# A new order for the last 30 microseconds of a fused four-layer kernel: last product by rows, bias products first, gamma and beta on VectorE in one go

## The chip, the cores and the metric

The kernel runs on one core of one Trainium2 chip, as one program that computes four layers for a batch of eight sequences of 512 rows and 512 features in float32. The metric is device time in microseconds (us); a kernel's time is the median of its runs, and lower is better. Engines are called as the profile calls them: PE is TensorE (PEld its weight loads), DVE is VectorE, ACT is ScalarE, POOL is GpSimd, SP is SyncE, from whose queue the transfers are issued.

## The reference, cut to what matters

The first two layers (a grid stencil step, and an attention block with its MLP) are not touched by the change. The third layer is an expert MLP with a norm, the fourth a low-rank response with a gate over the whole sequence:

```python
def L2(x, Wi, bi, Wo, bo, gamma, beta):            # weights of the sequence's expert
    h = gelu(x @ Wi + bi)                          # 512 x 2048
    r = h @ Wo + bo + x                            # 512 x 512
    y = (r - mean(r)) * rsqrt(var(r) + 1e-12)      # over the features of a row
    return y * gamma + beta

def L3(y, safety, U, V, safety_bias, gate_w1, gate_b1, gate_w2, gate_b2, resp_w, resp_b):
    basis = gram_schmidt(U) @ gram_schmidt(V).T
    pooled = y.mean(axis=rows)                     # one vector for the sequence
    h1 = relu(pooled @ gate_w1.T + gate_b1)
    strength = sigmoid(h1 @ gate_w2.T + gate_b2) * sigmoid(safety) * knob
    feats = (y @ basis) @ basis.T[:, :32]          # 512 x 32
    return y + strength * (feats @ resp_w.T + resp_b + safety_bias)
```

Strength needs the mean over all 512 rows of a sequence, so no row of a sequence's output can be finished before its last row has been normalised.

## The kernel before, in words

The whole program is one `fused_kernel`. Stages follow one another: grid, attention, and `mlp_stage` (L1145 on), which holds all that the change touches. `mlp_stage` runs sixteen steps `q` (L1713): steps 0 to 7 are the MLP of the second layer, one sequence each, steps 8 to 15 the expert MLP of the third. A sequence's 512 rows lie as 128 partitions times four rows (`R` = 4), so that its tile `xs[q]` is 128 x 4 x 512.

Both products of a step are Strassen-like schemes of seven block products in float32. Every product of a 128x128 weight tile with a moving tile of 256 columns shows in the profile as two passes. In `run` (L1463) the first product's seven blocks are made for each of four groups of hidden columns (`NG`), slots 0 to 27; the second product's seven blocks follow through `second` (L1536), each accumulated over all four groups in one PSUM tile, at slots 28, 32, ... 52. The block at slot 52 (`p4`, tile name `y_{q}_52`) is the last and is added to rows 2 and 3, columns 0 to 255, of x (`x_add(1, 0, p4)`). In `second` the loop over groups `g` is outside and the loop over the two row blocks `m` inside, so that both rows are complete only at its end.

The order on every engine is that of the Python code, kept by `pin`; nothing reorders it later. Work of other steps is woven in by `hooks`: `at(hooks, s, f, ...)` has f called at slot s. The fourth layer of sequence `q - 1` is made in this way during step q: `tail_norm` (L1600, normalises rows in place), `tail_turn` (L1618, PE transposes of 128x128 blocks and an ACT read that applies gamma and beta as columns and sums over the rows for the gate's mean), `tail_gamma` (L1609), `tail_feats` (L1640: features `pf`, and their copy `ft`), `gate` (L1652: `pg` and h1), `strength` (L1665: `pz`, a sigmoid and the product with the safety score), `add_beta` (on POOL), `tail_sum` (L1679: response `po`) and `tail_add` (L1689: the sum into x, and after rows 1 and 3 a store of two rows).

Sequence 15 has no step behind it. Its rows 0 and 1 are complete before the last block product and get norm, transposes, features and gamma at slots 49 to 55 (L1764 to L1770). Rows 2 and 3 are done behind the loop (L1773 to L1801): beta of rows 0, 1 on POOL; norm of rows 2, 3 together; the gate's products `pg` of the first half; transposes; gamma on DVE; features and gate alternating for the four column blocks; copies and h1 on DVE; beta of rows 2, 3 on POOL; for each row a response product `po` of two parts, `ft` with `rw` and a row of ones with the biases `rb`; strength; and four sums on DVE with two stores of 512 KB.

PSUM tiles come from two rings: tag `tr` with two buffers and tag `u` with six. `rstd_of` (L66) takes one DVE add and one power on POOL.

Of the kernel before, what the change touches and what calls it, by code (L numbers as in the profile page):

```python
# [24 lines left out]
R = 4  # L25
# [1119 lines left out]
def mlp_stage(tc, a, small, xp, io, wo8, x1d, ident, eidx, sigs, layernorm, rstd_of, phalf, wl3, g2, b1, first):  # L1145
# [19 lines left out]
    with ExitStack() as ctx:  # L1165
# [6 lines left out]
        def mm(out, lhsT, rhs, start, stop):  # L1172
            pin(nc.tensor.matmul(out, lhsT=lhsT, rhs=rhs, start=start, stop=stop))  # L1173

        def tp(out, src, idn=ident):
            pin(nc.tensor.transpose(out, src, idn))  # L1176

        def add(out, x, y, op=ALU.add):
            pin(nc.vector.tensor_tensor(out, x, y, op))  # L1179
# [283 lines left out]
        def run(q, hooks):  # L1463
# [9 lines left out]
            def act_quad(g, i, j):  # L1473

                return acts[g][:, 2 * j : 2 * j + 2, H * i : H * i + H]
# [60 lines left out]
            def second(s, A, B, each=None):  # L1536
                y = ps.tile([P, 2, H], F32, name=f"y_{q}_{s}", tag="u", bufs=6)
                for g in range(NG):
                    go(s + g)
                    if s == 28 and g == 2:  # L1540
                        s13(NG - 1)
                    for i in range(2):
                        for m in range(2):
                            mm(
                                y[:, m, :], A(g)[:, i, m * P : (m + 1) * P], B(g)[:, i, :],
                                g + i + m == 0, g + i + m == NG + 1,
                            )
                    if each:
                        each(g)
                return y  # L1550

            def x_add(i, j, t):
                o = quad(x, i, j)
                add(o, t, o)

            def b(i, j):
                return lambda g: quad(wo[g], i, j)
# [25 lines left out]
            add(yu, p7, yu)  # L1583
            x_add(1, 1, yu)
            x_add(1, 0, yu)
            p4 = second(52, lambda g: act_quad(g, 1, 1), b(1, 0))
            x_add(1, 0, p4)

        def t13(q, g):

# [46 lines left out]
                )  # L1637
                t["ys"][c] = y

        def tail_feats(q, rows):  # L1640
            ys = outs[q]["ys"]
            pf = ps.tile([P, P], F32, name=f"pf_{q}_{rows[0]}", tag="tr")
            for c in range(KC):
                for i, r in enumerate(rows):
                    mm(
                        pf[r * RK : (r + 1) * RK, :], wl3[:, c, :], ys[c][:, i, :],
                        c == 0, c == KC - 1,
                    )
            m = slice(rows[0] * RK, (rows[-1] + 1) * RK)
            pin(nc.vector.tensor_copy(outs[q]["ft"][m, :], pf[m, :]))  # L1650

        def gate(q):  # L1652

            pooled = outs[q]["pooled"]
            if len(pooled) > 1:
                add(pooled[0], pooled[0], pooled[1])
            pg = ps.tile([P, 1], F32, name=f"pg_{q}", tag="tr")
            for c in range(KC):
                mm(pg, gw1[:, c, :], pooled[0][:, c : c + 1], c == 0, c == KC - 1)
            h1 = small.tile([P, 1], F32, name=f"h1_{q}", tag="h1")  # L1660
            pin(nc.vector.tensor_scalar(h1, pg, 1.0 / S, gb1, ALU.mult, ALU.add))
            pin(nc.vector.tensor_scalar(h1, h1, 0.0, None, ALU.max))
            outs[q]["h1"] = h1

        def strength(q):  # L1665
            pz = ps.tile([P, 1], F32, name=f"pz_{q}", tag="tr")
            mm(pz, gw2, outs[q]["h1"], True, True)
            st = small.tile([P, 1], F32, name=f"st_{q}", tag="st")
            pin(nc.scalar.activation(st, pz, AF.Sigmoid, bias=gb2))
            add(st, st, sigs[:, q - NB : q - NB + 1], ALU.mult)  # L1670
            outs[q]["st"] = st
# [5 lines left out]
            gadd(x, x, beta[:, None, :].to_broadcast([P, R, D]))  # L1677

        def tail_sum(q, r):  # L1679
            last = q == NQ - 1  # L1680
            ft, m = outs[q]["ft"], slice(r * RK, (r + 1) * RK)
            po = outs[q]["po", r] = ps.tile(
                [P, D], F32, name=f"po_{q}_{r}", tag="u", bufs=6
            )
            mm(po, ft[m, :], rw[m, :], True, not last)
            if last:
                mm(po, ones[m, :], rb[m, :], False, True)

        def tail_add(q, r):  # L1689
            x, t = xs[q], outs[q]  # L1690
            pin(
                nc.vector.scalar_tensor_tensor(
                    x[:, r, :], t["po", r], t["st"], x[:, r, :], ALU.mult, ALU.add
                )
            )
            if r % 2:
                nc.sync.dma_start(
                    a["out"][q - NB].rearrange("(p r) f -> p r f", r=R)[:, r - 1 : r + 1, :],
                    x[:, r - 1 : r + 1, :],
                )  # L1700


        def at(hooks, s, f, *args):
            hooks.setdefault(s, []).append(lambda: f(*args))
# [8 lines left out]
        for q in range(NQ):  # L1713
# [50 lines left out]
            if q == NQ - 1:  # L1764
                half = range(0, 2)
                at(hooks, 49, tail_norm, q, half)
                for c in range(KC):
                    at(hooks, 51 + c, tail_turn, q, half, [c])
                at(hooks, 55, tail_feats, q, half)
                at(hooks, 55, tail_gamma, q, half)  # L1770
            run(q, hooks)

        q, half = NQ - 1, range(2, 4)  # L1773
        x, beta, t = xs[q], extra[q][1][2], outs[NQ - 1]
        gadd(x[:, 0:2, :], x[:, 0:2, :], beta[:, None, :].to_broadcast([P, 2, D]))
        tail_norm(q, half)
        pg = ps.tile([P, 1], F32, name=f"pg_{q}", tag="u", bufs=6)
        for c in range(KC):
            mm(pg, gw1[:, c, :], t["pooled"][0][:, c : c + 1], c == 0, False)
        tail_turn(q, half, range(KC))  # L1780
        tail_gamma(q, half)
        pf = ps.tile([P, P], F32, name=f"pf_{q}_2", tag="u", bufs=6)
        for c in range(KC):
            for i, r in enumerate(half):
                mm(
                    pf[r * RK : (r + 1) * RK, :], wl3[:, c, :], t["ys"][c][:, i, :],
                    c == 0, c == KC - 1,
                )
            mm(pg, gw1[:, c, :], t["pooled"][1][:, c : c + 1], False, c == KC - 1)
        m = slice(half[0] * RK, (half[-1] + 1) * RK)  # L1790
        h1 = small.tile([P, 1], F32, name=f"h1_{q}", tag="h1")
        pin(nc.vector.tensor_copy(t["ft"][m, :], pf[m, :]))
        pin(nc.vector.tensor_scalar(h1, pg, 1.0 / S, gb1, ALU.mult, ALU.add))
        pin(nc.vector.tensor_scalar(h1, h1, 0.0, None, ALU.max))
        t["h1"] = h1
        gadd(x[:, 2:4, :], x[:, 2:4, :], beta[:, None, :].to_broadcast([P, 2, D]))
        for r in range(R):
            tail_sum(q, r)
        strength(q)
        for r in range(R):  # L1800
            tail_add(q, r)  # L1801


# [86 lines left out]
```

## Time and profile before

| | |
|---|---|
| time, median of 3 runs | 2748.12 us (2746.18 to 2751.13) |
| time of the profiled execution | 2746.39 us |
| span of the profile | 2744.6 us |
| PE busy | 2693.7 us, 98% |
| DVE, ACT, POOL busy | 69%, 38%, 55% |
| mean granted clock of PE | 0.994 |
| begin of the last block product's first pass behind the transposes | 2714.03 us |
| last block product complete | 2722.59 us |
| first and last store of sequence 15 issued | 2739.48, 2740.8 us |

Times inside the profile count from the start of the span. The span covers the instructions of one execution; the time of that execution is 1.8 us longer. The granted clock is the share of its full speed that PE is given in a stretch of time. In the chain that ended last, each piece waited for the piece before it.

### The profile page before, as it was taken

The numbers are of one execution on the slowest core, as the hardware profiler recorded it, in microseconds if no ns is written. First come the engines' busy times: TensorE is split into PE (matmuls) and PEld (weight loads), VectorE is DVE, ScalarE is ACT, GpSimd is POOL, SyncE is SP. The second block draws the span as 40 slices with busy tenths as digits, with TensorE's granted clock in tenths as the row PEclk, the third lists the DMA queues.
The fourth block names the chain that finished last, engine by engine and source line by source line (L and its number), as shares of the span: only waits on it lengthen the run. The fifth ranks groups of instructions, "written<-read, shape, count | busy, mean of one in ns | idle before, by whom it ended". The sixth has DMA issues, their size and how long they took to land.

```text
span 2744.6 us, 39872 instructions
## 1 busy us (share of the span) xinstructions
PE 2693.7 (98%) x14662; PEld 2007.0 (73%) x14662; DVE 1899.7 (69%) x3506; ACT 1034.0 (38%) x2196; POOL 1505.3 (55%) x1091
## 2 busy tenths in 40 slices
PE   7999999999999998999999999999999999999998
PEld 4455555555555555888888888888888888888886
DVE  7888888888888655677656756665456566566564
ACT  2576767667667765211211211211121221221221
POOL 3455555555555653565555656646546636636633
PEclk9999999999999999999999999999999999999998
DMA  8765767666675544642543344253133143143120
GB/s 318 238 222 178 246 190 232 220 194 227 195 242 180 170 155 142 192 129 54 143 143 84 96 145 124 55 173 123 44 127 131 51 150 128 53 150 103 63 70 31
DMA packets 190208, 405.27 MB, mean 148 GB/s; under 512 B 24024, under 2 KB 28704, under 8 KB 183742
## 3 DMA queue, kind: packets, MB, share of 16 engines
q1 hardware_dynamic: 186202, 391.97, 42.7%
q0 software_dynamic: 3360, 10.68, 3.2%
q8 instruction: 117, 1.92, 0.3%
q14 instruction: 77, 0.63, 0.1%
q10 hardware_dynamic: 452, 0.07, 0.0%
HBM read 366.97 MB, written 31.50 MB: 145 GB/s over the span
## 4 chain that ended last, share of the span: by engine, by line
PE 92%; DVE 4%; ACT 2%; DMA 1%; issue 1%; SPq 0%; ACTq 0%; POOL 0%; DVEq 0%
PE u L1173 28%; PE y L1173 28%; PE tr L570 8%; PE s L567 5%; PE ctx L567 4%; PE pq L567 4%; PE pv L567 4%; PE o L567 4%; PE pk L567 3%; PE btr L1176 1%; DVE bt L1005 1%; PE xb L570 1%; DVE x L695 1%; PE ytr L1176 1%; ACT bt L1010 1%
## 5 line engine op out<-in xcount | busy, mean ns | idle before, releaser
L982 POOL TENSOR_TENSOR bt<-bt,mk 128x1024 f32<-128x1024 f32 x256 | 542.6, 2141 | 56.8 <-DMA bt<-in_bias 38.2
L1173 PE MATMUL y<-wo,act 128*128 128x256 f32 x2560 | 573.3, 380 | 0.0
L1173 PEld LDWEIGHTS y<-wo,act 128*128 128x128 f32 x2560 | 481.3, 190 | 70.0 <-issue 6.9
L1010 ACT ACTIVATE bt<-bt,mn 128x512 f32<-128x512 f32 x512 | 365.7, 716 | 78.6 <-DVE mn L1005 78.0
L570 PEld LDWEIGHTS tr<-ident,bt 128*128 128x128 f32 x2048 | 229.1, 141 | 153.0 <-issue 124.7
L1005 DVE CUSTOM_DVE_ANT_0 bt<-s,bt 128x512 f32<-128x512 f32 x512 | 330.8, 684 | 2.4 <-PE s L567 2.4
L1173 PE MATMUL u<-bt,wi 128*128 128x256 f32 x1440 | 330.5, 379 | 0.0
L1179 DVE TENSOR_TENSOR act<-u,u 128x512 f32<-128x512 f32 x256 | 173.3, 686 | 210.0 <-PE u L1173 132.6
L1173 PEld LDWEIGHTS u<-bt,wi 128*128 128x128 f32 x1440 | 273.5, 190 | 37.2
L570 PE MATMUL tr<-ident,bt 128*128 128x128 f32 x2048 | 276.2, 278 | 11.5 <-ACT pt L1033 9.4
L1173 PE MATMUL u<-tb,ws 128*128 128x256 f32 x1024 | 242.2, 379 | 0.0
L1033 ACT COPY pt<-tr 128x512 f32<-128x512 f32 x315 | 177.1, 581 | 159.6 <-PE tr L570 155.7
L1173 PE MATMUL y<-t,s 128*128 128x256 f32 x1024 | 234.2, 380 | 0.0
L1182 POOL TENSOR_TENSOR t<-wo,t 128x512 f32<-128x512 f32 x64 | 106.6, 1681 | 200.6 <-PE y L1173 200.5
L1173 PEld LDWEIGHTS u<-tb,ws 128*128 128x128 f32 x1024 | 194.3, 190 | 26.6 <-DVE tb L1179 0.2
L1031 DVE COPY pt<-tr 128x512 f32<-128x512 f32 x197 | 135.7, 689 | 112.7 <-PE tr L570 98.0
L1173 PEld LDWEIGHTS y<-t,s 128*128 128x128 f32 x1024 | 191.1, 190 | 24.1
L1493 ACT ACTIVATE act<-act,b 128x512 f32<-128x512 f32 x128 | 82.9, 712 | 292.9 <-DVE act L1179 292.9
L1493 ACT ACTIVATE act<-act,bi 128x512 f32<-128x512 f32 x128 | 83.8, 712 | 282.6 <-DVE act L1179 282.6
L1179 DVE TENSOR_TENSOR x<-y,x 128x512 f32<-128x512 f32 x96 | 64.5, 685 | 159.1 <-PE y L1173 105.2
L1179 DVE TENSOR_TENSOR u<-u,u 128x512 f32<-128x512 f32 x192 | 131.3, 684 | 58.2 <-PE u L1173 58.1
L567 PE MATMUL s<-kt,qt 32*128 32x512 f32 x1024 | 166.4, 640 | 2.5 <-DVE mn L1005 1.6
(316 smaller groups left out, 4250.1 us busy)
## 6 DMA issues: line engine op xcount, KB each, us to landing
bt<-in_bias SPq DMA_DIRECT2D x256, 512.0 KB
wo<-in_W SPq DMA_DIRECT2D x32, 1024.0 KB
wi<-in_Wi SPq DMA_DIRECT2D x32, 1024.0 KB
wo<-in_Wo_e SPq DMA_DIRECT2D x32, 1024.0 KB
wi<-in_W SPq DMA_DIRECT2D x28, 1024.0 KB
gq<-coef_q SPq DMA_DIRECT2D x21, 512.0 KB
x1d<-x SPq DMA_DIRECT2D x8, 1024.0 KB
x<-x1d SPq DMA_DIRECT2D x8, 1024.0 KB
```

Of the source, the lines that this page charges most:

```text
L567: pin(nc.tensor.matmul(out, lhsT=lhsT, rhs=rhs, start=start, stop=stop))
L570: pin(nc.tensor.transpose(out, src, ident))
L982: nc.gpsimd.tensor_tensor(bt, bt, mask[b, r][:, None, :].to_broadcast([P, 2, S]), ALU.add)
L1005: nc.vector.tensor_tensor_reduce(bt[:, i, :], ss[h], bt[:, i, :], -1.0, 3.0e38, ALU.add, ALU.min, mn)
L1010: nc.scalar.activation(bt[:, i, :], bt[:, i, :], AF.Exp, bias=mn, scale=-1.0, accum_out=sums[b, c, r][:, h : h + 1],)
L1031: pin(nc.vector.tensor_copy(pt[:, :, r % 2, :], tr))
L1033: pin(nc.scalar.copy(pt[:, :, r % 2, :], tr))
L1173: pin(nc.tensor.matmul(out, lhsT=lhsT, rhs=rhs, start=start, stop=stop))
L1176: pin(nc.tensor.transpose(out, src, idn))
L1179: pin(nc.vector.tensor_tensor(out, x, y, op))
L1182: pin(nc.gpsimd.tensor_tensor(out, x, y, op))
L1493: nc.scalar.activation(acts[g][:, k, :], acts[g][:, k, :], func, bias=bi[:, j : j + 1])
```

## The change

The end of step 15 is written anew as `last_row`, in the order in which rows become complete.

- The last block product runs row by row: the loop over `m` is outside, `last_row(m, y)` follows each, and each row has a PSUM tile of 128x256.
- Row 2 gets sum and norm behind the first half; row 3 behind the second.
- The transposes of rows 0, 1 for the third and fourth column block come one slot after the second, both at slot 53. Features of rows 0, 1 are moved behind the product, after row 2's transposes.
- The four bias products (`ones` with `rb`) open the accumulation of `po` ahead of row 3's transposes; the four products of `ft` with `rw` close it behind `pz`.
- Two PSUM tiles hold the transposes of rows 2 and 3 for two column blocks each, and one ACT read takes a column block of both rows.
- gamma and beta for all four rows are two DVE operations of 128x2048, behind row 3's transposes. POOL has no part in it.
- h1 (a Relu), the copy of `ft` and row 0's product with strength are on ACT; row 0's sum is on POOL, rows 1, 2, 3 are summed on DVE.
- Three stores from SP: rows 1 and 2, row 3, row 0.

For the other sequences `tail_sum`, `gate`, `strength` and `tail_feats` do what they did.

```diff
@@ -1583,8 +1583,21 @@
             add(yu, p7, yu)
             x_add(1, 1, yu)
             x_add(1, 0, yu)
-            p4 = second(52, lambda g: act_quad(g, 1, 1), b(1, 0))
-            x_add(1, 0, p4)
+            if q < NQ - 1:
+                p4 = second(52, lambda g: act_quad(g, 1, 1), b(1, 0))
+                x_add(1, 0, p4)
+            else:
+                for m in range(2):
+                    y = ps.tile([P, H], F32, name=f"y_{q}_52_{m}", tag="u", bufs=6)
+                    for g in range(NG):
+                        if g % 2 == 0:
+                            go(52 + 2 * m + g // 2)
+                        for i in range(2):
+                            mm(
+                                y, act_quad(g, 1, 1)[:, i, m * P : (m + 1) * P],
+                                b(1, 0)(g)[:, i, :], g + i == 0, g + i == NG,
+                            )
+                    last_row(m, y)
 
         def t13(q, g):
 
@@ -1637,9 +1650,9 @@
                 )
                 t["ys"][c] = y
 
-        def tail_feats(q, rows):
+        def tail_feats(q, rows, tag="tr", bufs=2):
             ys = outs[q]["ys"]
-            pf = ps.tile([P, P], F32, name=f"pf_{q}_{rows[0]}", tag="tr")
+            pf = ps.tile([P, P], F32, name=f"pf_{q}_{rows[0]}", tag=tag, bufs=bufs)
             for c in range(KC):
                 for i, r in enumerate(rows):
                     mm(
@@ -1652,8 +1665,6 @@
         def gate(q):
 
             pooled = outs[q]["pooled"]
-            if len(pooled) > 1:
-                add(pooled[0], pooled[0], pooled[1])
             pg = ps.tile([P, 1], F32, name=f"pg_{q}", tag="tr")
             for c in range(KC):
                 mm(pg, gw1[:, c, :], pooled[0][:, c : c + 1], c == 0, c == KC - 1)
@@ -1662,9 +1673,11 @@
             pin(nc.vector.tensor_scalar(h1, h1, 0.0, None, ALU.max))
             outs[q]["h1"] = h1
 
-        def strength(q):
+        def strength(q, also=None):
             pz = ps.tile([P, 1], F32, name=f"pz_{q}", tag="tr")
             mm(pz, gw2, outs[q]["h1"], True, True)
+            if also:
+                also(*range(R))
             st = small.tile([P, 1], F32, name=f"st_{q}", tag="st")
             pin(nc.scalar.activation(st, pz, AF.Sigmoid, bias=gb2))
             add(st, st, sigs[:, q - NB : q - NB + 1], ALU.mult)
@@ -1677,14 +1690,11 @@
             gadd(x, x, beta[:, None, :].to_broadcast([P, R, D]))
 
         def tail_sum(q, r):
-            last = q == NQ - 1
             ft, m = outs[q]["ft"], slice(r * RK, (r + 1) * RK)
             po = outs[q]["po", r] = ps.tile(
                 [P, D], F32, name=f"po_{q}_{r}", tag="u", bufs=6
             )
-            mm(po, ft[m, :], rw[m, :], True, not last)
-            if last:
-                mm(po, ones[m, :], rb[m, :], False, True)
+            mm(po, ft[m, :], rw[m, :], True, True)
 
         def tail_add(q, r):
             x, t = xs[q], outs[q]
@@ -1697,6 +1707,100 @@
                 nc.sync.dma_start(
                     a["out"][q - NB].rearrange("(p r) f -> p r f", r=R)[:, r - 1 : r + 1, :],
                     x[:, r - 1 : r + 1, :],
+                )
+
+        q15 = NQ - 1
+        z = {}
+
+        def last_row(m, y):
+            x, r, t = xs[q15], 2 + m, outs[q15]
+            gamma, beta = extra[q15][1][1:]
+            o = x[:, r, 0:H]
+            add(o, y, o)
+            st = small.tile([P, 6], F32, name=f"z_st_{r}", tag="ln2_st")
+            mv = z["mv", r] = small.tile([P, 2], F32, name=f"z_mv_{r}", tag="ln2_mv")
+            pin(nc.vector.bn_stats(st, x[:, r, :]))
+            pin(nc.vector.bn_aggr(mv, st))
+            rs = z["rs", r] = rstd_of(mv[:, 1:2], LN_EPS2, 1, "ln2", pin)
+
+            def scaled():
+                pin(
+                    nc.vector.tensor_scalar(
+                        x[:, r, :], x[:, r, :], mv[:, 0:1], rs, ALU.subtract, ALU.mult
+                    )
+                )
+
+            if m == 0:
+                scaled()
+                return
+            z["tr"] = [
+                ps.tile([P, 2, 2, P], F32, name=f"ytr_{q15}_2_{c}", tag="tr") for c in range(2)
+            ]
+            last_turn(0)
+            tail_feats(q15, range(0, 2), "u", 6)
+            for k in range(R):
+                po = t["po", k] = ps.tile([P, D], F32, name=f"po_{q15}_{k}", tag="u", bufs=6)
+                mm(po, ones[k * RK : (k + 1) * RK, :], rb[k * RK : (k + 1) * RK, :], True, False)
+            scaled()
+            last_turn(1)
+            pg = ps.tile([P, 1], F32, name=f"pg_{q15}", tag="u", bufs=6)
+            for c in range(KC):
+                mm(pg, gw1[:, c, :], t["pooled"][0][:, c : c + 1], c == 0, False)
+            cols, ys = extra[q15][2], []
+            pool = small.tile([P, KC], F32, name="z_pool", tag="pool")
+            for c in range(KC):
+                v = ap.tile([P, 2, P], F32, name=f"yT_{q15}_2_{c}", tag="tmp", bufs=4)
+                pin(
+                    nc.scalar.activation(
+                        v, z["tr"][c // 2][:, c % 2, :, :], AF.Identity, bias=cols[:, 1, c : c + 1],
+                        scale=cols[:, 0, c : c + 1], accum_out=pool[:, c : c + 1],
+                    )
+                )
+                ys.append(v)
+            tail_gamma(q15, range(R))
+            add(x, x, beta[:, None, :].to_broadcast([P, R, D]))
+            pf = ps.tile([P, P], F32, name=f"pf_{q15}_2", tag="u", bufs=6)
+            for c in range(KC):
+                for i in range(2):
+                    r = 2 + i
+                    mm(
+                        pf[r * RK : (r + 1) * RK, :], wl3[:, c, :], ys[c][:, i, :],
+                        c == 0, c == KC - 1,
+                    )
+                mm(pg, gw1[:, c, :], pool[:, c : c + 1], False, c == KC - 1)
+            h1 = small.tile([P, 1], F32, name=f"h1_{q15}", tag="h1")
+            pin(nc.scalar.activation(h1, pg, AF.Relu, bias=gb1, scale=1.0 / S))
+            pin(nc.scalar.copy(t["ft"][2 * RK :, :], pf[2 * RK :, :]))
+            t["h1"] = h1
+
+            def response(*rows):
+                for r in rows:
+                    m = slice(r * RK, (r + 1) * RK)
+                    mm(t["po", r], t["ft"][m, :], rw[m, :], False, True)
+
+            strength(q15, response)
+            out = a["out"][q15 - NB].rearrange("(p r) f -> p r f", r=R)
+            v = ap.tile([P, D], F32, name="z_r", tag="tmp", bufs=4)
+            pin(nc.scalar.mul(v, t["po", 0], t["st"]))
+            gadd(x[:, 0, :], x[:, 0, :], v)
+            for r in (1, 2, 3):
+                pin(
+                    nc.vector.scalar_tensor_tensor(
+                        x[:, r, :], t["po", r], t["st"], x[:, r, :], ALU.mult, ALU.add
+                    )
+                )
+            pin(nc.sync.dma_start(out[:, 1:3, :], x[:, 1:3, :]))
+            pin(nc.sync.dma_start(out[:, 3, :], x[:, 3, :]))
+            pin(nc.sync.dma_start(out[:, 0, :], x[:, 0, :]))
+
+        def last_turn(m):
+            for c in range(KC):
+                tp(
+                    z["tr"][c // 2][:, c % 2, m, :],
+                    xs[q15][:, 2 + m, c * P : (c + 1) * P],
                 )
 
@@ -1765,40 +1869,8 @@
                 half = range(0, 2)
                 at(hooks, 49, tail_norm, q, half)
                 for c in range(KC):
-                    at(hooks, 51 + c, tail_turn, q, half, [c])
-                at(hooks, 55, tail_feats, q, half)
-                at(hooks, 55, tail_gamma, q, half)
+                    at(hooks, (51, 52, 53, 53)[c], tail_turn, q, half, [c])
             run(q, hooks)
-
-        q, half = NQ - 1, range(2, 4)
-        x, beta, t = xs[q], extra[q][1][2], outs[NQ - 1]
-        gadd(x[:, 0:2, :], x[:, 0:2, :], beta[:, None, :].to_broadcast([P, 2, D]))
-        tail_norm(q, half)
-        pg = ps.tile([P, 1], F32, name=f"pg_{q}", tag="u", bufs=6)
-        for c in range(KC):
-            mm(pg, gw1[:, c, :], t["pooled"][0][:, c : c + 1], c == 0, False)
-        tail_turn(q, half, range(KC))
-        tail_gamma(q, half)
-        pf = ps.tile([P, P], F32, name=f"pf_{q}_2", tag="u", bufs=6)
-        for c in range(KC):
-            for i, r in enumerate(half):
-                mm(
-                    pf[r * RK : (r + 1) * RK, :], wl3[:, c, :], t["ys"][c][:, i, :],
-                    c == 0, c == KC - 1,
-                )
-            mm(pg, gw1[:, c, :], t["pooled"][1][:, c : c + 1], False, c == KC - 1)
-        m = slice(half[0] * RK, (half[-1] + 1) * RK)
-        h1 = small.tile([P, 1], F32, name=f"h1_{q}", tag="h1")
-        pin(nc.vector.tensor_copy(t["ft"][m, :], pf[m, :]))
-        pin(nc.vector.tensor_scalar(h1, pg, 1.0 / S, gb1, ALU.mult, ALU.add))
-        pin(nc.vector.tensor_scalar(h1, h1, 0.0, None, ALU.max))
-        t["h1"] = h1
-        gadd(x[:, 2:4, :], x[:, 2:4, :], beta[:, None, :].to_broadcast([P, 2, D]))
-        for r in range(R):
-            tail_sum(q, r)
-        strength(q)
-        for r in range(R):
-            tail_add(q, r)
 
 # ---- launch: one core; inputs are laid out here and nothing more ----
```

## The prediction

> **What bounds the kernel now.** I read four views of the profile, from the whole to the end. The page's first parts say that TensorE (PE) is busy for 98% of a span of 2744.6 us, and the chain of work that ended last lies on PE for 92%. The built order of instructions on each engine is the same in both kernels up to the last product of step 15 (the block `y_52`), but for line numbers. So about 2714 us of the span stay as they are, and only the last 30 us can change. The second view is that chain over the end:
>
> ```profile
> 2719.65 1.00 PE pf L1173 x16
> 2720.65 1.94 PE y L1173 x8
> 2722.59 0.02 issue
> 2722.61 0.70 DVE x L1179
> ...
> 2725.33 0.72 POOL ln_r L71
> ...
> 2726.07 0.56 DVE x L85
> ...
> 2726.76 0.85 PE ytr L1176 x2
> ...
> 2732.91 0.57 PE pf L1173 x4
> 2733.47 0.52 PE pg L1173 x2
> 2733.99 3.11 PE po L1173 x16
> ...
> 2739.42 1.32 DVE x L1692 x2
> ```
>
> The columns are start, length and piece of the chain. The last product ends at 2722.59; then a chain of dependent steps runs through all engines: x gets the product, norm (4.0 us), transposes, features and gate alternating on PE (2729.64 to 2733.99), sixteen passes of the response `po`, strength, four sums. In that chain nothing overlaps.
>
> The third view, busy time by stretch, is cut where the granted clock can change (PE's busy time is the second number, the clock is the third from the end):
>
> ```profile
> 50.07:53.48 3.41, 3.41 (x33) 3.41 (x32) 1.82 (x4) 1.15 (x2) 0.00 (x0) 1.00 0.49 194
> 53.48:56.90 3.42, 3.42 (x18) 3.42 (x18) 2.11 (x8) 0.00 (x0) 1.05 (x1) 0.50 0.88 282
> ...
> 1063.82:1067.23 3.41, 2.37 (x20) 1.93 (x18) 2.94 (x7) 2.19 (x6) 1.20 (x1) 1.00 0.02 5
> ...
> 2722.69:2726.10 3.41, 0.67 (x6) 0.58 (x6) 2.45 (x7) 0.00 (x0) 2.62 (x2) 1.00 0.00 0
> 2726.10:2729.51 3.41, 2.37 (x8) 1.26 (x8) 0.97 (x2) 1.52 (x5) 0.00 (x0) 0.50 0.02 5
> 2729.51:2732.93 3.42, 3.42 (x21) 2.17 (x22) 1.23 (x1) 0.89 (x4) 1.95 (x1) 0.50 0.00 0
> ```
>
> PE has 0.67 us of work in the stretch of the norm (2722.69); from its end on it runs at half clock, to 2736.34. The rows from elsewhere are for the question of when that happens. Four passes of `pf` take 0.57 us there; sixteen take 1.00 at full clock (2719.65), so four take 0.25.
>
> The fourth view is the timeline and the groups by shape, for prices:
>
> ```profile
> 2722.41 0.95 PE L1173 MATMUL pg<-pool,gw 128*128 128x1 f32 x8
> 2738.01 2.73 DVE L1692 SCALAR_TENSOR_TENSOR x<-po,st,x 128x512 f32<-128x512 f32 x4
> 2739.48 1.65 SPq L1697 DMA_DIRECT2D out<-x  x2
> ...
> L1613 DVE TENSOR_TENSOR x<-x,gamma 128x2048 f32<-128x2048 f32 x7 | 23.5, 3363 | 0.0
> L1613 DVE TENSOR_TENSOR x<-x,gamma 128x1024 f32<-128x1024 f32 x2 | 2.4, 1216 | 2.6 <-PE ytr L1176 2.6
> L245 DVE TENSOR_TENSOR e<-ce,f 128x2048 f32<-128x2048 f32 x1 | 2.3, 2292 | 0.0
> ```
>
> **The change part by part.** All times below are on the scale of the profiled execution.
>
> *Last product.* The order is `m` outside `g`, but it is still 32 passes at 0.2165 us (1.73 for 8 in the chain). The first two transposes of rows 0 and 1 stand where they stood, so I start at 2714.03, the begin of `y_52`. 32 passes take 6.92, the two remaining pairs of transposes 0.44 (0.22 each): row 2 is complete at 2717.93 and row 3 at 2721.39. Before it was 2722.59: `pf` (1.00 and 0.2 of switching) has left the front of it. **−1.2 us.** No DMA moves here: the stores of step 14 are issued at 2707 as before.
>
> *Row 2* gets its sum and norm from 2717.93 to about 2720.9 under row 3's product (slack 0.5 us). It costs nothing; without this cover it would be the 3.0 us of the next part.
>
> *Row 3's norm.* A sum of 128x256 (0.42, the row of the 128x256 sums of `hT`), one bn_stats (0.71), one aggregate (0.18), 0.18 for v, 0.07 + 0.72 for the power on POOL, 0.56 for the scaling, and gaps of 0.02 to 0.03: 2.97, ending at 2724.36. Before: 4.03. **−1.05 us.** VectorE copies `ft` of rows 0, 1 ahead of the scaling and waits for `pf`; PE does transposes (0.44) and `pf` (1.0 to 1.2) from 2721.39, so the copy ends at about 2723.35, while POOL's power ends at 2723.7. Slack 0.3 us; queued behind are scaling and all that follows, so a later `pf` would count one to one.
>
> *PE in the meantime.* The four bias products of `po` take 1.07 (the eight passes at 2699.57 in the chain of step 14), to 2724.1. PE then waits 0.3 us for the scaling. Four transposes of row 3: 0.66 to the last result, 2725.1.
>
> *The clock.* Does it still fall? In the stretch 2722.69 to 2726.10 the new kernel has 1.4 us of `pf` and bias products, 0.66 of transposes and 0.8 of `pg`: 2.85 us, an estimate from the rows above. Elsewhere the half clock followed on stretches with 1.06 and 1.33 us of PE work and not on those with 2.28 and 2.37. But it also followed on the stretch at 50.07 with 3.41 us, all of the embedding's products (L145, 8 columns wide): narrow products seem not to count, and `pg` is one column wide. Without it 2.05 us are left, nearer to 2.28 than to 1.33: I take the full clock. The Trainium skill speaks against it ("TensorE: Matmul & The Clock Gate", Part 4): a PE transpose doesn't count as busy in the same way; then only 1.4 us count, and the clock falls. The trace doesn't bear that out: the stretch at 1063.82 holds nothing but transposes on PE, 2.37 us, and the clock stays. By the row the clock costs nothing; by the rule it falls at 2726.1, at +1.3 us (rival B).
>
> *ScalarE path.* The first read of the turned tile starts 0.5 us after row 3's first transpose: 2724.95. Four reads at 0.56 (2727.70 to 2728.26 before), the last with its accumulator done 0.64 after its start: 2727.27. PE's features and gate for each column block (0.25 + 0.2) fit under the pitch of 0.56; the last ends at 2727.8. Relu (0.26), `pz` (0.33), sigmoid (0.27) with hand-overs: strength ready for VectorE at 2728.9. The `ft` copy (0.29) lies beside `pz`. The response's eight passes (1.07) run behind `pz`, to 2729.6. Before, from scaling to strength: 11.1 us; now 4.5. The skill advises relu, add and mul on VectorE ("ScalarE: Activation LUTs", Rules for kernel authors). The rows: 0.26 for a one-column ScalarE read against 0.22 + 0.15 for VectorE's two. On VectorE they would stand in front of beta and cost 0.3 to 0.7 of its path, which is the longer one, as follows.
>
> *Gamma and beta, all rows, on VectorE.* They wait for row 3's transposes (they overwrite x): 2725.1. Two ops over 128x2048. Bounds: 2.29 (L245, POOL idle) and 3.36 (L1613 with POOL at work). POOL has nothing from 2723.7 on, so 2.29 each: to **2729.7**. This is later than strength by 0.8: VectorE, not PE, now sets the end. Before, half of this lay under the last product, and beta on POOL.
>
> *Last sums.* Strength times safety, then the first sum starts 0.27 later (2737.74 to 2738.01): 2729.98. Rows 1, 2 are done 1.41 later (2739.42 less 2738.01): 2731.39. Row 3: 2732.05. Row 0: ScalarE's product 0.72, then POOL's sum 1.27 (alone) to 1.80 (beside VectorE's), done at 2732.1 to 2732.6.
>
> *Stores.* Before: issued at 2739.48, 0.06 behind the second sum; data for 2.6 us, end of span at 2744.6, 5.12 later. Now the first 512 KB go at 2731.45, the rows 3 and 0 behind it while data still flow: the third store's data can start at about 2733.4 and the first's end near 2733.6. So the bytes set the end again: 2731.45 + 5.12 = **2736.6**.
>
> *Sum.* Start of the first store 2739.48 to 2731.45: −8.0 us of 2744.6. By term: −1.2 product, −1.05 norm, and −5.8 from scaling to first store (13.0 now less in clock, order and bias products: 2726.62 to 2739.48 is 12.86, 2724.36 to 2731.45 is 7.09). The profiled execution took 2746.39 with a span of 2744.6 and would take 2738.4. The median shown is 2748.12, 1.7 above; less 8.0: **2740.1** (−0.29%).
>
> **The rivals.**
> A, forecast: VectorE sets the end at full clock, −8.0.
>
> B, the clock halves all the same. For it: 2.05 is below every stretch that held, and at 2729.51 even 3.42 us of busy PE did not bring the full clock back. Against: the row of transposes. Price, if it falls at 2726.1: the last three pairs of features and gate at 1.09 instead of 0.45, so strength at 2731.0 and the first sum at 2731.3, +1.3. Falling earlier would need a stretch that takes in more of the dense product; falling at 2727 costs +0.7. So −6.7: 2741.4; bounds −7.3 and −6.1.
>
> C, gamma and beta cost 3.36 each as in steps 9 to 15. For it: most L1613 rows; against: POOL is at work in those. +2.1: −5.9, 2742.2.
>
> D, slower than before: the phase of the clock's stretches. They run free, by the same page (Part 1); no run here shows it yet. The half clock comes in pieces of 3.41 us, and near the changes of stage (53 to 145 us and 1050 to 1090 us) there are stretches with PE work between 2.15 and 2.7 us. If another phase closes more of them, each costs about 1.7 us (half of 3.41), anywhere in the kernel. It decides from 5 more closed windows on; six give +2.2: 2750.3. Against: three runs before lie within 5 us.
>
> E, the change saves only the product's reorder, since each later piece waits for `pf` behind PE: then −3: 2745.1. Against: 0.3 us of slack, and no DMA in between.
>
> **How the numbers follow.** A 0.66, B 0.17, C 0.07, E 0.06, D 0.04. The likeliest gives 2740.1. A's own range is 2738 to 2742: the medians move by 1 to 2 us, and sizes by 1 us. The range takes B and C in: 2737.0 to 2744.0, which leaves out D, E and the far edges. The bound of what a measurement can tell is 0.2%, 5.5 us: A is beyond it in most draws (0.60 of 0.66), B and C in 0.17 of 0.24; faster 0.77, within 0.19, slower 0.04.
>
> **What would show it.** Clock 1.00 up to about 2729; row 3's product ending near 2721.4; `pf` of rows 0, 1 behind it; VectorE's gamma and beta at 2.29 each, and the first sum waiting for VectorE and not for strength; the first store near 2731.5. A half clock from 2724 or 2726, gamma of 3.3 us, or a scaling that waits for the `ft` copy would make it wrong.

## The result, and the profile after

| | before | changed |
|---|---|---|
| time, median | 2749.7 us (20 runs, 2746.18 to 2752.0) | 2744.99 us (20 runs, 2740.75 to 2748.7) |
| ratio | | 0.9982, 95% interval 0.9976 to 0.9989 |
| span of the profile | 2744.6 us | 2744.7 us |
| first pass of the last block product | 2713.86 us | 2717.69 us |
| from there to the end of the span ("end stretch") | 30.75 us | 27.04 us |

The changed kernel is faster by 0.18%, or 4.9 us (0.0018 of 2749.7). The forecast was 8.0 us and a time between 2737.0 and 2744.0; the time measured lies above that range, and its distance from before is just inside the 0.2% that was given as the bound of what can be told.

The two spans are equal although the time differs, because the work ahead of the end stretch, the same instructions in both, took 3.8 us longer in this profile. That part is left to the end of this text; until then times count from the first pass of the last block product (2713.86 before, 2717.69 after), where it doesn't matter. On that scale the forecast was 22.7 us, and 3.7 of the 8.0 us came.

The chain that ended last, of the changed kernel (start, length, piece):

```profile
2720.02 5.20 PE y L1173 x24
2725.21 0.02 issue
2725.24 0.43 DVE x L1179
...
2727.46 0.56 DVE x L1731
2728.02 0.04 issue
2728.06 0.66 PE ytr L1176 x4
2728.72 0.79 PE pg L1173 x8
2729.51 0.34 PE pf L1173 x4
2729.85 0.31 PE pg L1173 x2
...
2732.48 0.58 PE pz L1173 x2
2733.06 2.10 PE po L1173 x8
2735.16 0.73 DVE x L1791
```

Up to the transposes all is as forecast. Then PE is in the chain without a break, and the eight closing passes of `po` take 2.10 us, where eight took 1.07 in step 14 of the kernel before:

```profile
2699.57 1.07 PE po L1173 x8
```

Busy time by stretch says why (PE's busy time is the second number, the clock the third from the end):

```profile
2725.24:2728.65 3.41, 3.05 (x34) 1.85 (x32) 2.19 (x6) 0.05 (x1) 0.55 (x1) 1.00 0.02 5
2728.65:2732.04 3.39, 3.39 (x33) 2.54 (x31) 3.25 (x2) 2.24 (x8) 0.00 (x0) 1.00 0.00 0
2732.04:2735.45 3.41, 2.69 (x11) 1.01 (x10) 1.80 (x3) 1.13 (x4) 0.00 (x0) 0.50 0.00 0
```

The forecast asked about a stretch from 8.83 to 12.24 on the common scale. In this profile the stretches are cut elsewhere, at 7.55, 10.96 and 14.35. The clock held behind the first of these rows and fell behind the second, right before `pz`, after 3.39 us in which PE was never idle. The timeline of the last operations:

```profile
2728.76 2.29 DVE L1626 TENSOR_TENSOR x<-x,gamma 128x2048 f32<-128x2048 f32 x1 [0.75 <-PE ytr L1176]
...
2731.08 2.29 DVE L1179 TENSOR_TENSOR x<-x,beta 128x2048 f32<-128x2048 f32 x1
...
2733.39 0.16 DVE L1179 TENSOR_TENSOR st<-st,sigs 128x1 f32<-128x1 f32 x1
2735.10 0.69 ACT L1787 ACTIVATE z_r<-po,st 128x512 f32<-128x512 f32 x1 [1.74 <-PE po L1173]
2735.14 2.07 DVE L1791 SCALAR_TENSOR_TENSOR x<-po,st,x 128x512 f32<-128x512 f32 x3 [1.59 <-PE po L1173]
2735.86 1.26 POOL L1182 TENSOR_TENSOR x<-x,z_r 128x512 f32<-128x512 f32 x1 [8.44 <-ACT z_r L1787]
2736.58 0.33 SPq L1795 DMA_DIRECT2D out<-x  x1
```

VectorE is through with beta at 2733.37 and has strength at 2733.55, and then waits 1.59 us for `po`. The first store is at 2736.58, or 18.9 on the common scale; 17.6 was forecast. But from it to the end of the span are 8.1 us, where there were 5.1 before. SyncE's own waits, and the rows of the program's last line in the changed kernel (durations in ns, min/median/max, then first and last start):

```profile
SPq L1958 <- PEq L1958: 3.3, 2, 2.8
...
L1958 POOLq DRAIN  x3: 46/107/8085, 2735.8 to 2744.5; - x3
L1958 SPq DRAIN  x3: 7/7/7, 2741.3 to 2744.2; - x3
```

and the same rows before, with POOL's last operation there:

```profile
2730.98 2.34 POOL L1182 TENSOR_TENSOR x<-x,beta 128x1024 f32<-128x1024 f32 x1 [4.95 <-DVE x L1613]
...
L1886 POOLq DRAIN  x3: 46/107/9165, 2730.9 to 2744.3; - x3
L1886 SPq DRAIN  x3: 7/7/7, 2743.8 to 2744.1; - x3
```

All engines meet at a barrier at the end of the program, each behind a drain of its own work. SyncE, which waits for the stores, drains at 2741.3 in the changed kernel, then no engine does any work for 2.6 us. The view puts this wait down to PE, which had drained long before (its longest drain took 2.5 us from 2732.8). The late one is POOL: its drain began at 2735.8 and took 8.1 us, to 2743.9, that is 6.8 us beyond the end of its last sum (2735.86 + 1.26 = 2737.12). Before, it is the same 6.8 us (2730.9 + 9.17 = 2740.1, last work done at 2733.32), but there the stores ended later and hid it.

### The profile page after: what moved, and what is told of

Its sections match the earlier page's. It is cut to its first block, busy times and chain, and to the rows that moved or that the text cites. A ratio compares the mean times of both kernels' runs of the same rounds, so it can differ in the third digit from the quotient of the medians.

```text
span 2744.7 us, 39871 instructions
## 1 busy us (share of the span) xinstructions
PE 2694.8 (98%) x14662; PEld 2005.6 (73%) x14662; DVE 1906.5 (69%) x3504; ACT 1034.7 (38%) x2199; POOL 1501.9 (55%) x1091
## 4 chain that ended last, share of the span: by engine, by line
PE 93%; DVE 3%; ACT 1%; DMA 1%; issue 0%; SPq 0%; ACTq 0%; POOL 0%; DVEq 0%
PE u L1173 28%; PE y L1173 28%; PE tr L570 8%; PE s L567 5%; PE ctx L567 4%; PE pq L567 4%; PE pv L567 4%; PE o L567 4%; PE pk L567 3%; PE btr L1176 1%; PE l L251 1%; DVE bt L1005 1%; ACT bt L1010 1%; DVE x L695 1%; PE xb L570 1%; PE ytr L1176 1%
## 5 line engine op out<-in xcount | busy, mean ns | idle before, releaser
L1179 DVE TENSOR_TENSOR x<-y,x 128x512 f32<-128x512 f32 (+1 forms) x97 | 64.6, 680 | 158.1 <-PE y L1173 104.2
```

## The experiments

Two theories had to be told apart from their rivals: that POOL's drain ends the program (against: three stores end late by themselves), and that the sums waited for `po` at half clock (against: VectorE's gamma and beta set the end, as forecast). All end stretches are from the first pass of the last block product. (Two of the expectations count from its place in the chain, 0.16 us later, and so give 30.6 and 26.9 for 30.75 and 27.04.)

### The changed kernel again

No edit.

> The changed kernel once more, as the neighbour of the others on the same chip. Measured is the end stretch: from the first pass of the last block product to the end of the span (before 30.6 us, changed 26.9 us in the first profile). Theory (POOL's drain at the end of the program sets the end, and the clock fell before pz and po): POOL's drain ends 6.8 us behind POOL's last sum, SyncE is through with the stores 2 to 3 us earlier, end stretch 25.5 to 27. Rival (three stores with a slow end of their own): SyncE itself is through only shortly before the span's end. If the half clock comes at another place because the clock's stretches run free, po's closing products take 1.1 us instead of 2.1 and the first store is 1 us earlier, but the end stretch shrinks by as much only if POOL's sum moves too. The part ahead of the stretch is longer by about 1.7 us for each further 3.41 us at half clock.

Time 2745.61 us, ratio 0.9982 (0.9975 to 0.9990). End stretch 27.05 us; first store at 18.89; SyncE drained at 23.58; POOL's last sum ended at 19.45 and its drain at 26.24. All of it is within 0.01 us of the first profile, and the clock fell at the same place, before `pz`. The end stretch is a far sharper measure than the time.

### All sums on VectorE

```diff
-            v = ap.tile([P, D], F32, name="z_r", tag="tmp", bufs=4)
-            pin(nc.scalar.mul(v, t["po", 0], t["st"]))
-            gadd(x[:, 0, :], x[:, 0, :], v)
-            for r in (1, 2, 3):
+            for r in (1, 2, 3, 0):
```

> Row 0's sum on VectorE behind rows 1, 2, 3; no ScalarE product and no POOL sum at the end. Theory (POOL's drain): POOL's last work is then row 3's power, about 9 us earlier, its drain is hidden under the stores; VectorE takes 0.66 us more, the last store goes 0.5 us later; end stretch 2.3 us shorter than the changed kernel's (about 24.5 at the same clock). Rival (the stores end late of themselves): the end stretch is the changed kernel's or 0.5 us longer. Time against before: 0.26% faster by the theory, 0.17% by the rival.

Time 2740.34 us, ratio 0.9970 (0.9959 to 0.9982). POOL's last work and the drains of this run:

```profile
2722.03 0.56 POOL L71 TENSOR_TENSOR ln_r<-ln_v,mhalf 128x1 f32<-128x1 f32 x1 [2.90 <-DVE ln_v L69]
...
L1955 POOLq DRAIN  x3: 46/107/7380, 2722.0 to 2737.9; - x3
L1955 SPq DRAIN  x3: 7/7/7, 2737.3 to 2737.6; - x3
```

POOL's drain ends at 2729.4, again 6.8 us behind its last work, and is hidden under the stores; the span ends 0.8 us after SyncE's drain. End stretch 25.32: 1.7 us less than the changed kernel, where 2.3 were expected. The clock accounts for what is missing: here it fell at 12.9 and not at 14.35, in the middle of features and gate, and strength came 0.9 us later (16.6 and not 15.7), although up to there the instructions are those of the changed kernel. In spite of that and of 0.66 us more on VectorE the end is earlier. The rival, no gain, is out.

### POOL last in the kernel before

```diff
         for r in range(R):
             tail_add(q, r)
+        late = small.tile([P, 1], F32, name="late", tag="late", bufs=1)
+        gadd(late, x[:, 3, 0:1], x[:, 3, 0:1])
```

> The kernel before with one more POOL operation of one column, behind the last sum on VectorE; nothing waits for it. Theory (POOL's drain takes 6.8 us from its last work, whatever that is): POOL ends about 2741.0 on the scale of the profile before, its drain 2747.8, where SyncE is through at 2743.8: end stretch +3.9 us (34.5), time +0.14%. Rival (the drain goes by the size of the last operation, or the drain in the changed kernel was late for another reason): 0.2 us of work leaves a short drain, end stretch within 0.5 us of the 30.6 before, time the same.

Time 2753.61 us, ratio 1.0015 (1.0008 to 1.0022).

```profile
2745.07 0.19 POOL L1182 TENSOR_TENSOR late<-x 128x1 f32<-128x1 f32 x1 [8.39 <-DVE x L1692]
...
L1888 POOLq DRAIN  x3: 46/107/7008, 2745.0 to 2752.6; - x3
L1888 SPq DRAIN  x3: 7/7/7, 2747.9 to 2752.3; - x3
```

An addition of one column, 0.19 us long, makes the kernel slower by 4 us. No work waits for it: the second store follows the first by 1.3 us, as before. Its drain ends at 2752.0 (2745.0 + 7.0), 6.8 us behind it; SyncE had drained at 2747.9. The end stretch is 35.64, 4.9 longer than before: 4.1 are the drain, 0.8 the clock, which in this run fell so that `pz` was slow too. The drain doesn't go by the size of the last operation: it is 6.8 us behind 128x1024, 128x512 and one column alike.

### Response of rows 0 and 1 early

```diff
             scaled()
+            response(0, 1)
             last_turn(1)
...
-            strength(q15, response)
+            strength(q15, lambda *rows: response(2, 3))
```

`response` is defined ahead of its first call.

> The changed kernel with the response products of rows 0 and 1 ahead of row 3's transposes, in the pause of TensorE there; only those of rows 2 and 3 stay behind pz. Theory (the four sums waited for po at half clock, not for VectorE's gamma and beta nor for strength): first sum 1.2 to 1.4 us earlier, POOL's sum and with it its drain too, end stretch 1.2 us shorter than the changed kernel's at the same clock; at full clock 0.4 us. Rival (VectorE's gamma and beta set the end, as forecast): the first sum stays where it was, 0.1 us behind beta, and the end stretch is the same; it is 0.2 us longer if the products push row 3's transposes back.

Time 2744.43 us, ratio 0.9982 (0.9974 to 0.9991). Timeline:

```profile
2731.45 2.07 PE L1173 MATMUL po<-rw,ft 32*128 32x512 f32 x4
2731.55 0.26 ACT L1682 ACTIVATE st<-pz,gb 128x1 f32<-128x1 f32 x1 [0.39 <-PE pz L1173]
...
2732.04 0.75 DVE L1793 SCALAR_TENSOR_TENSOR x<-po,st,x 128x512 f32<-128x512 f32 x1
...
2733.55 1.41 DVE L1793 SCALAR_TENSOR_TENSOR x<-po,st,x 128x512 f32<-128x512 f32 x2 [0.76 <-PE po L1173]
```

The first sum (row 1) comes at 16.6, 0.9 us earlier, and right behind strength, not behind beta. So the sums had waited for `po`. But the four closing passes of rows 2 and 3 take as long as the eight did (2.07 and 2.10): the passes of different rows, each on its own 32 partitions, run side by side, and to take half of them away shortens nothing. Row 2 waits for its product, and the first store stays at 18.9. Strength itself is 0.7 us later, since the early products push row 3's transposes back by half a microsecond and the last gate products fell to half clock. The end stretch is shorter all the same, 26.22: ScalarE's product and POOL's sum of row 0 came 0.82 us earlier, and the end by exactly that. It followed POOL, not the stores.

### Gate products 128 columns wide

```diff
-            pg = ps.tile([P, 1], F32, name=f"pg_{q15}", tag="u", bufs=6)
+            pg = ps.tile([P, P], F32, name=f"pg_{q15}", tag="u", bufs=6)
...
-                mm(pg, gw1[:, c, :], pool[:, c : c + 1], False, c == KC - 1)
+                mm(
+                    pg, gw1[:, c, :], pool[:, c : c + 1].to_broadcast([P, P]), False, c == KC - 1
+                )
```

The four products of rows 0, 1 are widened in the same way, and h1 reads column 0.

> The changed kernel with one edit: the gate's products pg of step 15 take their one column 128 times (broadcast), so that each pass streams 128 columns and not one; the result is in column 0 as before. The weight loads (0.15 us a pass) bound them either way. Theory (products of one column don't count for the clock, which is why it falls while TensorE looks busy): the clock stays at 1.00 to the end of po, pz takes 0.33 and the eight closing passes 1.1 us instead of 2.1, the first sum starts at 16.3 instead of 17.4, end stretch 25.8. Rival (the clock falls for another reason, such as the pauses before pz): half clock from before pz as in the changed kernel, end stretch 27.0 to 27.4.

Time 2744.78 us, ratio 0.9982 (0.9976 to 0.9989).

```profile
2727.46:2730.87 3.41, 3.05 (x30) 1.95 (x22) 2.41 (x2) 2.02 (x7) 0.21 (x1) 1.00 0.00 0
2730.87:2734.28 3.41, 3.06 (x26) 1.79 (x24) 2.88 (x3) 1.06 (x5) 0.00 (x0) 1.00 0.00 0
2734.28:2737.70 3.42, 0.43 (x4) 0.00 (x0) 2.07 (x3) 0.69 (x1) 1.26 (x1) 1.00 0.20 81
...
2733.26 0.38 PE L1173 MATMUL pz<-h,gw 128*128 128x1 f32 x2 [0.35 <-ACT h L1780]
...
2733.57 1.14 PE L1173 MATMUL po<-rw,ft 32*128 32x512 f32 x8
...
2734.77 2.07 DVE L1796 SCALAR_TENSOR_TENSOR x<-po,st,x 128x512 f32<-128x512 f32 x3 [0.64 <-PE po L1173]
```

The same products with more columns keep the full clock to the end of `po`. But the stretches are cut elsewhere than in the changed kernel's profile, and that alone could have saved the clock. (The cuts are counted in steps of 3.41 us from the changes of the clock, which lie whole multiples of that apart.) The run with all sums on VectorE settles it: it is cut at the same places, 9.53 and 12.94 on the common scale, and up to strength it has the changed kernel's instructions, with the narrow products:

```profile
2722.37:2725.78 3.41, 3.05 (x32) 2.14 (x24) 2.42 (x2) 2.03 (x7) 0.21 (x1) 1.00 0.00 0
2725.78:2729.19 3.41, 3.06 (x20) 2.16 (x19) 2.71 (x2) 0.81 (x5) 0.00 (x0) 0.50 0.00 0
```

In both runs PE is busy for 3.05 us of the stretch up to 12.94; behind it the clock is half with products of one column and full with products of 128. `po` takes 1.14 and not 2.10. The wider passes cost 0.5 us on the way, of which the faster `pz` gives back some, so the first sum is 0.6 us earlier (16.84) and the end stretch 26.43. The expected 1.2 had left out what the wide passes cost. At full clock, too, VectorE waits for `po`, 0.64 us.

### A reordered end

```diff
             last_turn(1)
+            response(0, 1)
...
-            strength(q15, response)
+            strength(q15, lambda *rows: response(2, 3))
...
-            for r in (1, 2, 3):
+            for r in range(R):
...
-            pin(nc.sync.dma_start(out[:, 1:3, :], x[:, 1:3, :]))
-            pin(nc.sync.dma_start(out[:, 3, :], x[:, 3, :]))
-            pin(nc.sync.dma_start(out[:, 0, :], x[:, 0, :]))
+            pin(nc.sync.dma_start(out[:, 0:2, :], x[:, 0:2, :]))
+            pin(nc.sync.dma_start(out[:, 2:4, :], x[:, 2:4, :]))
```

The gate's products of rows 0, 1 stand ahead of `last_turn(1)` and no longer behind it, and `response` is defined ahead of both. ScalarE's product and POOL's sum of row 0 are gone.

> The changed kernel with: all four sums on VectorE in the order of rows 0 to 3, two stores of 512 KB; the gate's products of rows 0, 1 ahead of row 3's transposes; the response products of rows 0, 1 behind them, so that only those of rows 2 and 3 stay behind pz. End stretch from the first pass of the last block product (before 30.7, changed 27.0, sums on VectorE alone 25.3). Theory (POOL's drain, then po behind pz are what is late): the first sum starts at 15.9 with strength, the first store goes at 17.4 and not 18.9, POOL's drain ends at 16.5 under it, end stretch 22.7. Rival (response products behind pz still hold all sums, since the first sum waits for the last of them): first sum at 17.4, end stretch 24.5.

Time 2742.62 us, ratio 0.9978 (0.9970 to 0.9987). Timeline of its last steps:

```profile
2730.45 1.13 PE L1173 MATMUL po<-rw,ft 32*128 32x512 f32 x4
...
2730.86 0.16 DVE L1179 TENSOR_TENSOR st<-st,sigs 128x1 f32<-128x1 f32 x1
2731.12 2.73 DVE L1790 SCALAR_TENSOR_TENSOR x<-po,st,x 128x512 f32<-128x512 f32 x4
2732.55 0.33 SPq L1794 DMA_DIRECT2D out<-x  x1
```

End stretch 23.07, 4.0 less than the changed kernel and 7.7 less than before. That is 0.4 longer than expected: the first sum starts at 16.5, not 15.9, since strength too is later. The four sums run without a pause behind strength; rows 0 and 1 cover the products of rows 2 and 3. The clock stayed full to 18.3 here, cut within half a microsecond of the changed kernel's profile (14.8 and, in its second profile, 14.6, against 14.35). The likely reason is that the response products of rows 0, 1, 512 columns wide, now lie among features and gate; no run took them away alone.

### Gamma and beta split again

The reordered end, and in addition:

```diff
+            if m == 0:
+                tail_gamma(q15, range(0, 2))
+                gadd(x[:, 0:2, :], x[:, 0:2, :], beta[:, None, :].to_broadcast([P, 2, D]))
...
-            tail_gamma(q15, range(R))
-            add(x, x, beta[:, None, :].to_broadcast([P, R, D]))
+            tail_gamma(q15, range(2, R))
+            add(x[:, 2:4, :], x[:, 2:4, :], beta[:, None, :].to_broadcast([P, 2, D]))
```

> As f1, and in addition gamma of rows 0, 1 on VectorE and their beta on POOL under the last block product, as in the kernel before; behind row 3's transposes only rows 2 and 3 are left for VectorE (2.4 us instead of 4.6). If gamma and beta in one go set the start of the sums (the forecast's reason), the first sum comes up to 2.3 us earlier than in f1, with strength. Theory: strength comes at 15.7 by way of ScalarE and TensorE anyway, beta ends at the same time in f1, so f2 gains at most 0.3 us: end stretch 22.5.

Time 2742.02 us, ratio 0.9972 (0.9961 to 0.9984). End stretch 23.08, first sum at 16.50, both as without the split (22.5 was expected). VectorE has 2.2 us less to do behind the transposes and nothing moves: gamma and beta in one go cost nothing, since strength is later.

### Both together

The reordered end with the split and the wide gate products.

> f2 and the wide gate products of f3 together, meant as the best version. By the theories of both: first sum at 15.5, the closing products of rows 2, 3 done at 16.2, first store at 17.0, end stretch 22.0, time 0.31% below before. If the clock falls all the same: as f2.

Time 2741.57 us, ratio 0.9974 (0.9964 to 0.9983). End stretch 23.55, 0.5 us worse. The clock was full already, so the wide passes only cost: strength at 16.7 instead of 16.2. The expectation (22.0) was wrong in taking the wide passes as free.

### More runs of the reordered end and of the changed kernel

> f1 again, with more runs, beside the changed kernel on the same chip. Its end stretch was 23.1 us, 4.0 shorter than the changed kernel's and 7.7 shorter than before. If the whole time follows the end stretch: 0.28% below before (ratio 0.9972), 0.15% below the changed kernel. If the part ahead of it, which varies by 1 to 5 us with the pieces at half clock, hides this: ratio as the changed kernel's, 0.998.

> The changed kernel again, for f1. End stretch 27.0 us with POOL's drain 6.8 us behind its last sum, as twice before; if the clock's pieces fall otherwise, up to 0.8 us less. Time by the end stretch alone: 0.135% below before (3.7 us of 2749), ratio 0.9987, inside the first interval (0.9976 to 0.9989).

The reordered end: 2740.43 us, ratio 0.9963 (0.9949 to 0.9977), end stretch 23.08. The changed kernel: 2745.01 us, ratio 0.9981 (0.9974 to 0.9989), end stretch 27.04. The intervals hold what the end stretches alone give for the reordered end (7.7 of 2749, ratio 0.9972) and just hold it for the changed kernel (3.7, 0.9987). The reordered end is faster than the kernel before. Against the changed kernel its end stretch is 4.0 us shorter in both of its profiles and its median 4.6 us lower, though the two intervals overlap a little.

## Why the prediction was wrong

Taken by its own steps, on the common scale (forecast times less 2713.86):

- *Last product*, −1.2 us: right. 8.71 us to its end before, 7.51 after.
- *Row 2* hidden, and *row 3's norm* 2.97 us: right, 2.81 measured. POOL's power of one column took 0.56 us, where 0.72, from two columns, was taken.
- *Gamma and beta*, 2.29 each with POOL idle: right, both 2.29; done at 15.7 where 15.8 was forecast.
- *The clock*: the forecast took the stretches to be cut where they had been cut before, asked about one of them (8.83 to 12.24) and left the products of one column out of the count. That these count for little or nothing is borne out by the two runs at equal cuts. Where the cuts fall was not in its hands: the first profile had none near 12.24. The run with all sums on VectorE was cut at 12.94, with about 1.7 us of work other than the gate's in the stretch, where the forecast counted 2.05 in its own, and there the clock fell. So that it held to 14.35 was luck of the cut as much as a right count. The step of the forecast that was wrong is that the stretch with features and gate was not asked about. The profile before had the warning, and the forecast quoted it for rival B: at 2729.51 features and gate kept PE busy for 3.42 us at half clock and did not bring the full clock back. What transposes count for was not tested further; the profile before has 2.37 us of them that kept the full clock (1063.82) and 2.37 us that did not bring it back (2726.10).
- *ScalarE path*: a pair of features and gate was set at 0.25 + 0.2 us, by scaling down runs of sixteen and eight passes. Alternating, a pair takes 0.34 + 0.31. Features and gate were done at 14.45 where 13.94 was forecast, and `pz`, behind the fall of the clock, took 0.58 where 0.33 was taken. Together they ate the slack of 0.8 us that strength was to have: it came at 15.7 together with beta.
- *The response's eight passes*: forecast done at 15.7, measured 17.4. They were the last to arrive, so VectorE did not set the start of the sums: the first came at 17.45 where 16.1 was forecast, and this is the first 1.3 us of the miss. The passes ended 1.7 us late: 0.5 from the pairs, 0.25 from `pz` and 1.0 from their own half clock. Without the fall of the clock they would have ended near 16.2 (an estimate, 17.4 less 1.0 and 0.25), still behind strength, which VectorE had ready at 15.87. Rival B had about this price for a fall at 12.24; in the first profile what it says on features and gate did not happen, and in the run with all sums on VectorE it did for the last two pairs.
- *Stores*, "so the bytes set the end again": this is the step that failed. The first store's bytes were followed and the end set at 5.12 us behind it. SyncE was through 4.68 us behind the first store, which would have been an end at 5.5. POOL, given the last sum of row 0, held the barrier 2.6 us longer. No rival had it, although its row is in the profile before: a drain of 9.2 us on POOL, hidden by 3.7 us of stores behind it. The 0.4 us left over goes with the third store: from the first store to SyncE's drain it is 4.2 to 4.3 us in the profiles with two stores and 4.7 in those with three, whether POOL has the last sum or not. Why a third store costs that is not shown.

The sum: 22.7 forecast, + 1.3 (clock and pairs, seen in the first store) + 0.4 (third store) + 2.6 (POOL's drain) = 27.0, as measured. Of the 8.0 us forecast 3.7 are left in the end stretch. The time measured is close to the number of rival E (2745.1), but by chance: its reason, row 3's pieces waiting behind `pf`, did not occur, since the scaling started right behind POOL's power (2727.43, 2727.46). The gamma of 3.36 us of rival C did not occur either.

The time says 4.9 (interval 3.0 to 6.6), the end stretch 3.7. Part of this is the clock in the kernel before: in the run with the late POOL operation the same code had its clock fall so that strength came 0.84 us later than in the first profile. The rest is inside the interval; what it is, if it is anything, stays open.

*Rival D*, the phase of the clock's stretches, didn't make the kernel slower, but is seen: in the kernel before the clock fell at 12.2 in one profile and at 11.2 in the one with the late POOL operation. In the twelve profiles the work ahead of the end stretch, the same instructions each time, took 2712.8 to 2717.9 us, and had 13.7 to 27.3 us at half clock by the trace's record of the clock. The kernel before was seen at 2713.9 with 20.5 us and, with the late POOL operation, at 2717.2 with 27.3. A line through all twelve has 0.34 us of time for a microsecond at half clock, 1.2 us for a piece of 3.41, where 1.7 was assumed. Single profiles lie up to 1.3 us off that line. This is argued from the fit, not from an edit.

## What to carry to other kernels

Look at the drains at the end of the program as at any other work: an engine whose last operation is cheap can still be the one that ends last, so in a kernel like this one POOL's last operation should end at least 6.8 us before the last store has landed, which is 7.6 us ahead of the end of the span. When a forecast says that a stall goes, ask of every later stretch, and not only of the one where the stall was, what the clock will do with the work that now lies in it; here many products of one column left TensorE busy, and at half clock. Prices of short groups of products are to be taken from rows with the same alternation, not scaled down from long runs.

## What had not been expected of the hardware

- POOL's drain at the end of the program lasted 6.8 us beyond its last operation in all twelve profiles, whatever that operation was (128x1024, 128x512, one column). What POOL does in that time the traces don't show. The drains of PE, VectorE and ScalarE in the changed kernel ended within 0.2 us of their last work.
- TensorE with 3.39 us of busy time in 3.39 us lost its full clock. With equal cuts and 3.05 us of busy time in 3.41 in both, it lost it with the gate's products at one column and kept it with 128.
- Four passes of 512 columns for two rows (32 partitions each) took 2.07 us at half clock and 1.13 at full clock, eight for four rows 2.10 and 1.14.
